# Layer 0 attention: row maxima carried by VectorE's 32x32 transpose and four small DMAs, in place of a TensorE transpose and a subtraction

## The chip, the cores and the metric

The kernel runs on one core of one Trainium2 chip. The metric is the device time of one execution in microseconds. Before the change it is 1144.48 us, the median of three runs (1144.44 to 1144.59).

The engines are named as in the profile: PE is TensorE's matrix multiplication and PEld its load of weights, DVE is VectorE, ACT is ScalarE, POOL is GpSimd, and SP is the engine whose queue issues most DMAs. A name such as L702 is line 702 of the kernel.

## What is computed

A transformer of two layers over x of 4 sequences x 512 tokens x 256 features, in float32. Layer 0 is causal attention with 16 heads of size 16, and then a feed-forward part that weighs the two best of eight experts for each output feature. Layer 1 is attention over the batch axis and a gated feed-forward part with 4-bit weights. The change touches layer 0's attention alone:

```python
qkv = einsum('bsd,od->bso', layernorm(x), w_project)      # 16 heads of 16, 512 keys
att = einsum('bhqd,bhkd->bhqk', q, k) / sqrt(16)
att = where(causal, -1e9, att)                            # a query sees keys up to its own
att = softmax(att, axis=-1)                               # needs the greatest score of each row
out = einsum('bhqk,bhkd->bhqd', att, v)
x = x + einsum('bsd,od->bso', out, w_out)
```

## The kernel before

The 512 tokens of a sequence are cut into 4 blocks j of 128. Queries and keys lie feature-major in one tile `qk[partition, g, block, s, token]`. The 16 heads are 4 groups g of 4 heads h, head h of a group lies in the band of partitions 32h to 32h+31, and s is the sequence. Places 0 to 3 of the block axis hold the keys of the four blocks; places 4 and 5 hold the queries of block j at place 4 + j % 2. In a band the 16 features lie at rows 4 to 19. Row i (0 to 3) of the keys of group i is 1 and the other rows outside the features are 0; the rows of the queries outside the features start at 0. These rows are set by GpSimd: once for block 0 (L496, a copy of a 0/1 mask spread over 4x512 columns), for later blocks by `blank` (L491), and for the queries by two fills with 0 (L500, and L521 in `blanks`).

The attention is worked through in 44 batches (j, s, groups): 4 batches of four groups for j = 0, 8 of two groups for j = 1, 16 of one group for j = 2, and 16 of one group for j = 3. Each batch has these steps:

- `greatest(n)`, L683: the scores with queries along partitions, into four PSUM tiles (one for each head h), by matmuls over the 32 rows of a band, four bands at a time.
- `mask(n)`, L696 and L702: a bf16 product adds -1e30 at later keys, and four VectorE reductions take each row's maximum into `maxes` (128 queries x head x group).
- `shift(n)`, L712 and L715: TensorE transposes `maxes` into a PSUM tile, so that row 32h + g holds the maxima of head h of group g along the columns. VectorE then subtracts this whole tile from the queries of the batch's groups. Row g of the queries now holds minus the maximum, and since the keys of group g have 1 in that row, the next product gives score minus maximum.
- `powers(n)`, L731, L740 and L750: the scores again, now with keys along partitions, over the same 32 rows, so that the maximum is already taken off. ScalarE takes the exponential, and GpSimd clears later keys in the last block.
- `mixed(n)`, L767: the product with the values, into a PSUM tile of the pool `ps_mm` (one buffer, which the transposed maxima use too), copied out by ScalarE.
- `divided`: the division by the sum, the projection and the addition to x.

The scores of both kinds take their four tiles from `ps_sc`, a pool of five buffers. So `powers(n)` can write its second tile only when the reductions of batch n+1 have freed theirs.

The main loop emits for batch n: `greatest(n+1)`, `shift(n)`, `mask(n+1)`, other work, `mixed(n-1)`, `powers(n)`, other work. "Other work" is taken by `fill` from streams of pieces: projections of later blocks, and the whole feed-forward part of layer 0 (L249 router and expert products on TensorE; L386 to L441 the choice of the two best, L365 to L367 additions, all on VectorE). How much is taken is fixed while the program is written out, from a cost that each piece states, and not from real times. TensorE, VectorE, ScalarE and GpSimd then keep that order. SP keeps it only up to batch 3; after that its order is set by the scheduler's priorities, and the four steps of a batch have a raised one.

SP issues, in the early batches, the DMAs that move projected queries and keys from `stage` to `qk` (L564, eight for each half block, 64 KB each) and the loads of the weights `rw` and `ew` of the experts (256 KB each). A DMA waits for an earlier DMA of the same of eight semaphores, eight DMAs back.

At the start, TensorE runs ten matmuls on an identity (L831) while x arrives. GpSimd sets the rows of `qk`, builds two small constants, and takes the inverse roots for the first layer norm (L649).

Of the kernel before, what the change touches and what calls it, by code (L numbers as in the profile page):

```python
# [8 lines left out]
F32 = mybir.dt.float32  # L9
# [3 lines left out]
ALU = mybir.AluOpType  # L13
# [3 lines left out]
P = 128  # L17
# [4 lines left out]
NBLK = 4  # L22
# [10 lines left out]
def tile_transformer(  # L33
# [18 lines left out]
    nc = tc.nc  # L52
# [23 lines left out]
    ident = const.tile([P, P], F32, name="ident")  # L76
# [9 lines left out]
    mask32 = const.tile([P, 32], F32, name="mask32")  # L86
# [16 lines left out]
    b2 = w_ffn0.enter_context(tc.tile_pool(name="f0_2", bufs=2, side="right"))  # L103
# [360 lines left out]
    with ExitStack() as l0:  # L464
        w0 = l0.enter_context(tc.tile_pool(name="w_l0", bufs=1))
        a1 = l0.enter_context(tc.tile_pool(name="l0_1", bufs=1))
# [3 lines left out]
        ps_mm = l0.enter_context(tc.tile_pool(name="l0_mm", bufs=1, space=PSUM))  # L470
# [5 lines left out]


        qk = w0.tile([P, 4, NBLK + 2, NS, P], F32, name="qk")
        maxes = [w0.tile([P, 4, 32], F32, name=f"mx{i}") for i in range(2)]

        va = w0.tile([P, NBLK * NS * NH0 * 17 + 15], F32, name="va")
        per_block = NS * NH0 * 17
# [2 lines left out]
        def blank(j, i):  # L485

            if i == 4:
                to = va.shape[1] if j == NBLK - 1 else (j + 1) * per_block
                nc.gpsimd.memset(va[:, j * per_block : to], 1.0)
            else:  # L490
                nc.gpsimd.tensor_copy(  # L491
                    qk[:, i, j].rearrange("p s q -> p (s q)"),
                    mask32[:, i : i + 1].to_broadcast([P, 512]),
                )

        nc.gpsimd.tensor_copy(  # L496
            qk[:, :, 0].rearrange("p g s q -> p g (s q)"),
            mask32[:, :4].unsqueeze(2).to_broadcast([P, 4, 512]),
        )
        nc.gpsimd.memset(qk[:, :, NBLK].rearrange("p g s q -> p g (s q)"), 0.0)  # L500

        ident_h = w0.tile([P, P], BF16, name="ident_h")
        nc.gpsimd.tensor_copy(ident_h, ident)
# [3 lines left out]
            out=later, in_=later, compare_op=ALU.is_ge, fill=NEG,  # L507
# [3 lines left out]
        rows = b1.tile([P, 12, P], BF16, tag="part", name="rows")  # L511
        sel = rows[:, :8]
        bp = rows[:, 8:].rearrange("p i q -> p (i q)")

        def blanks(xn):

            after = b2.tile([P, 1], F32, tag="rs_v", name="after")
            nc.gpsimd.tensor_copy(after, xn[:, 3, 0:1])
            for i in range(2):
                nc.gpsimd.memset(maxes[i], 0.0)  # L520
            nc.gpsimd.memset(qk[:, :, NBLK + 1].rearrange("p g s q -> p g (s q)"), 0.0)  # L521

        def split_biases():

# [24 lines left out]
        def project(j, xT, half, stage, i):  # L549

            at = 256 * (1 - i) + 128 * half
            ps = ps_dn.tile([P, 512], F32, tag="dn", name=f"qk_ps{j}_{half}_{i}")
            for hc in range(2):
                nc.tensor.matmul(  # L554
                    ps, lhsT=wp[:, hc, at : at + P],
                    rhs=xT[:, hc].rearrange("p s q -> p (s q)"), start=hc == 0, stop=hc == 1,
                )
            (nc.scalar.copy if j or not half else nc.vector.tensor_copy)(stage[:, i], ps)
            if i:
                to = 4 + j % 2  # L560
                for r in range(8):
                    h = 32 * (r % 4)
                    eng = nc.scalar if j == 0 and r % 2 else nc.sync
                    eng.dma_start(  # L564
                        out=qk[h + 4 : h + 20, 2 * half + r // 4, j : to + 1 : to - j].rearrange(
                            "p i s q -> p i (s q)"
                        ),
                        in_=stage[16 * r : 16 * r + 16],
                    )
# [95 lines left out]
        for j in range(NBLK):  # L665
            n = (4, 2, 1, 1)[j]
# [5 lines left out]
        def queries(j, g):  # L672
            return qk[:, g, 4 + j % 2]

        def greatest(n):

            j, s, gs = batches[n]
            nk = (j + 1) * P
            tiles = [ps_sc.tile([P, 512], F32, tag="sc", name=f"s1_{n}_{h}") for h in range(4)]
            for b, g in enumerate(gs):  # L680
                for h in range(4):
                    r = slice(32 * h, 32 * h + 32)
                    nc.tensor.matmul(  # L683
                        tiles[h][:, b * nk : (b + 1) * nk].rearrange("p (c k) -> p c k", k=P),
                        lhsT=queries(j, g)[r, s], rhs=qk[r, g, : j + 1, s, :],
                        start=b == 0, stop=False,
                    )
            open_scores[n] = tiles

        def mask(n):  # L690

            j, s, gs = batches[n]
            nk, nb = (j + 1) * P, len(gs)
            tiles = open_scores.pop(n)
            for ps in tiles:
                nc.tensor.matmul(  # L696
                    ps[:, : nb * nk].rearrange("p (b k) -> p b k", b=nb)[:, :, j * P :],
                    lhsT=ident_h, rhs=later.unsqueeze(1).to_broadcast([P, nb, P]),
                    start=False, stop=True,
                )  # L700
            for h, ps in enumerate(tiles):
                nc.vector.tensor_reduce(  # L702
                    maxes[n % 2][:, h, gs[0] : gs[0] + nb],
                    ps[:, : nb * nk].rearrange("p (b k) -> p b k", b=nb), AX.X, ALU.max,
                )

        def shift(n):


            j, s, gs = batches[n]  # L710
            ps = ps_mm.tile([P, P], F32, tag="mm", name=f"mxT_{n}")
            nc.tensor.transpose(ps, maxes[n % 2].rearrange("p h g -> p (h g)"), ident)  # L712
            g, nb = gs[0], len(gs)
            q = qk[:, g : g + nb, 4 + j % 2, s, :]
            nc.vector.tensor_tensor(  # L715
                q, q, ps.unsqueeze(1).to_broadcast([P, nb, P]), ALU.subtract
            )

        powers_of = {}

        def powers(n):

            j, s, gs = batches[n]
            nk, nb = (j + 1) * P, len(gs)
            tiles = [ps_sc.tile([P, 512], F32, tag="sc", name=f"s2_{n}_{h}") for h in range(4)]
            for b, g in enumerate(gs):
                for c in range(j + 1):
                    at = b * nk + c * P
                    for h in range(4):
                        r = slice(32 * h, 32 * h + 32)  # L730
                        nc.tensor.matmul(  # L731
                            tiles[h][:, at : at + P],
                            lhsT=qk[r, g, c, s, :], rhs=queries(j, g)[r, s],
                            start=True, stop=True,
                        )
            powers_of[n] = []
            for pair in range(2):
                pt = a3.tile([P, 2, 512], F32, tag="pt", name=f"pt_{n}_{pair}")
                for i in range(2):
                    nc.scalar.activation(  # L740
                        pt[:, i, : nb * nk], tiles[2 * pair + i][:, : nb * nk], AF.Exp, scale=0.25
                    )

                last = pt[:, :, : nb * nk].rearrange("p h (b k) -> p h b k", b=nb)[
                    :, :, :, j * P :
                ]
                pattern = [[0, 2], [0, nb], [1, P]]
                if nb == 1:
                    last, pattern = last[:, :, 0], [[0, 2], [1, P]]
                nc.gpsimd.affine_select(  # L750
                    out=last, in_=last, compare_op=ALU.is_ge, fill=0.0,
                    base=0, pattern=pattern, channel_multiplier=-1,
                )
                powers_of[n].append(pt)
# [74 lines left out]
        ps = ps_mm.tile([P, 4, P], F32, tag="mm", name="idle")  # L829
        for i in range(5):  # L830
            nc.tensor.matmul(  # L831
                ps, lhsT=ident, rhs=ident.unsqueeze(1).to_broadcast([P, 4, P]),
# [2 lines left out]
        load_x(1)  # L835
        nc.sync.dma_start(out=wo, in_=w_out.rearrange("(k p) o -> p k o", p=P))
        xn = normed_by_twos()
        blanks(xn)
        xT = a1.tile([P, 2, NS, P], F32, tag="xT0", name="xT0_0")
        for piece in inputs_T(0, xn, xT):  # L840
            pass
# [25 lines left out]
        for piece in inputs_T(1, second[0], xT):  # L867
            pass
        greatest(0)
        mask(0)  # L870
        inputs = {1: Stream(projections(1, xT))}
        done = blanked = 0
        fold = Stream(fold_pieces())
# [4 lines left out]
        for n in range(NBT):  # L878
            j, s, gs = batches[n]
            if n in (1, 7):  # L880
                to = 2 if n == 1 else 3
# [5 lines left out]
            with tc.high_priority(offset=AHEAD):  # L887
                if n + 1 < NBT:
                    greatest(n + 1)
                shift(n)  # L890
                if n + 1 < NBT:
                    mask(n + 1)

            fill(PE=(2.0, 2.0, 1.8, 1.6)[j], DVE=2.6)
            with tc.high_priority(offset=AHEAD):
# [73 lines left out]
    with ExitStack() as l1:  # L969
# [3 lines left out]
        for kv, i in [(slice(None), slice(HPK + 1, HPK + 2))] + [  # L973
            (slice(kv, kv + 1), slice(0, HPK + 1)) for kv in range(NKV)
        ]:
            for hc in range(2):
                tc.keep_in_program_order(
                    nc.sync.dma_start(
                        out=wqkv[:, hc, kv, i], in_=w_qkv[hc * P : (hc + 1) * P, kv, i]
# [239 lines left out]
        for p in range(-1, NP):  # L1219
            j, kv = divmod(p, NKV)  # L1220
# [59 lines left out]
    with ExitStack() as f1:  # L1280
# [186 lines left out]
        f, k = firsts  # L1467
# [3 lines left out]
        for i in range(NBLK * NJ):  # L1471
            j, jj = divmod(i, NJ)
# [12 lines left out]
            e, g = eg[:, 0], eg[:, 1]  # L1485
# [147 lines left out]
```

## Time and profile before

The profiled execution took 1144.61 us. Its span, from the first to the last instruction, is 1142.9 us.

| stretch (us) | what runs there | PE busy | DVE busy | POOL busy |
|---|---|---|---|---|
| 20 to 120 | blocks 0 and 1, projections, loads of expert weights | 97.88 of 100 | 68.13 | 34.12 |
| 120 to 160 | block 2 begins, experts fill in | 40.00 of 40 | 34.96 | 8.81 |
| 160 to 360 | blocks 2 and 3 with experts | 197.06 of 200 | 185.20 | 36.04 |
| 360 to 1143 | rest of the experts, layer 1 | 760.33 of 783 | 543.27 | 152.69 |

A busy PE in these rows is one on which some matmul is in flight; it includes time in which the next matmul waits behind the last, so 100% doesn't say that TensorE alone sets the time. The granted clock is 1.00 in every stretch. The steps of the change run from 22 us (first L683) to 366 us (last L731).

| step | instruction | count | mean or median ns |
|---|---|---|---|
| L683 | matmul over 32 rows, 128 to 512 columns | 512 | 287 to 639 |
| L696 | mask product, bf16, 128 columns a group | 176 | 219 at one group |
| L702 | reduction of 384 or 512 columns | 176 | 548, 681 |
| L712 | transpose of the maxima | 44 | 327 |
| L715 | subtraction | 44 | 281, 418 or 690 for one, two, four groups |
| L731 | matmul over 32 rows, 128 columns | 1280 | 287 |
| L767 | product with the values | 1280 | 276 |

### The profile page before, as it was taken

The page shows a single profiled execution, that of the slowest core. Times are in us where ns is not written, and L with a number is a line of the kernel's source. Part 1 is how long each engine was busy: PE and PEld are TensorE (multiplying, and loading weights), DVE is VectorE, ACT ScalarE, POOL GpSimd, SP SyncE. Part 2 cuts the span into 40 slices and gives each one's busy share as a digit, 9 for nine tenths or more (in the row PEclk, how much of TensorE's full clock was granted, in tenths as well). Part 3 has the DMA queues.
Part 4 walks back from the last instruction along what each step waited for, and adds up shares of the span by engine and source line. Part 5 has one row for each costly group of instructions (what it writes and reads, how often), then busy time and mean ns, then how long its engine had stood idle before and what let it go on. Part 6 is the DMA issues. An engine that isn't in the chain of part 4 may idle for free.

```text
span 1142.9 us, 19523 instructions
## 1 busy us (share of the span) xinstructions
PE 1113.0 (97%) x7474; PEld 716.1 (63%) x7474; DVE 844.6 (74%) x1856; ACT 509.8 (45%) x1190; POOL 247.1 (22%) x319
## 2 busy tenths in 40 slices
PE   9999999999999999999999999999999999999998
PEld 5666555555555445555555556656787788888885
DVE  6676989999988962867772695577479877778665
ACT  1445545565555543444444353344324444444442
POOL 8322221211112000000000000000064544353433
PEclk9999999999999999999999999999999999999999
DMA  4450110000000400000000001242001002002000
GB/s 133 113 130 2 21 20 1 2 1 2 1 2 1 156 29 1 1 1 1 1 1 0 1 1 38 65 111 65 20 1 45 30 19 74 1 19 74 18 3 19
DMA packets 30510, 34.92 MB, mean 31 GB/s; under 512 B 4280, under 2 KB 21432, under 8 KB 30416
## 3 DMA queue, kind: packets, MB, share of 16 engines
q1 hardware_dynamic: 29600, 32.49, 10.4%
q10 hardware_dynamic: 816, 1.18, 0.4%
q8 instruction: 59, 0.97, 0.3%
q14 instruction: 35, 0.29, 0.1%
HBM read 23.17 MB, written 6.29 MB: 26 GB/s over the span
## 4 chain that ended last, share of the span: by engine, by line
PE 69%; DVE 22%; ACT 3%; issue 2%; POOL 1%; SPq 1%; DMA 1%; DVEq 0%; POOLq 0%; ACTq 0%
PE qk_ps L1029 10%; PE lg_ps L249 9%; PE o L1120 8%; PE eo L249 7%; PE eg L955 7%; PE gu_first L955 5%; PE s L731 3%; PE yx L1336 3%; DVE mx L702 3%; PE s L683 3%; PE av L767 2%; PE yy L1336 2%; DVE it L1412 2%; DVE th L1411 2%; PE qk_ps L554 2%
## 5 line engine op out<-in xcount | busy, mean ns | idle before, releaser
L1029 PE MATMUL qk_ps<-xT,wqkv 128*128 128x512 f32 x320 | 148.7, 599 | 3.5 <-ACT v L1015 1.7
L249 PE MATMUL lg_ps<-rw,xT 128*128 128x512 f32 x256 | 122.5, 601 | 1.4 <-ACT xT L996 0.3
L249 PE MATMUL eo<-ew,xT 128*128 128x512 f32 x256 | 121.5, 600 | 0.8 <-ACT lg L312 0.5
L1120 PE MATMUL o<-wpj,oT 128*128 128x256 f32 x512 | 119.1, 382 | 0.0
L750 POOL TENSOR_SCALAR_AFFINE_SELECT pt<-pt 128x256 f32<-128x256 f32 (+2 forms) x88 | 62.4, 716 | 246.6 <-ACT pt L740 246.5
L1120 PEld LDWEIGHTS o<-wpj,oT 128*128 128x128 f32 x512 | 96.0, 190 | 27.0 <-issue 13.5
L1029 PEld LDWEIGHTS qk_ps<-xT,wqkv 128*128 128x128 f32 x320 | 59.1, 190 | 73.2 <-issue 58.4
L702 DVE TENSOR_REDUCE mx<-s 128x1 f32<-128x384 f32 (+3 forms) x176 | 100.4, 632 | 0.0
L740 ACT ACTIVATE pt<-s 128x512 f32<-128x512 f32 (+1 forms) x176 | 84.1, 564 | 35.8 <-PE s L731 35.8
L182 POOL TENSOR_TENSOR ln_rs<-rs_v,minus_half 128x4 f32<-128x4 f32 x12 | 13.6, 1131 | 366.2 <-DVE rs_v L181 366.2
L338 ACT ACTIVATE part<-eo,c 128x256 f32<-128x256 f32 x128 | 53.6, 472 | 84.6 <-PE eo L249 74.7
L1523 ACT COPY gu_first<-eg 128x512 f32<-128x512 f32 x28 | 16.0, 570 | 134.2 <-PE eg L955 129.9
L249 PEld LDWEIGHTS lg_ps<-rw,xT 128*128 128x128 f32 x256 | 46.1, 190 | 46.1 <-issue 37.3
L249 PEld LDWEIGHTS eo<-ew,xT 128*128 128x128 f32 x256 | 46.1, 190 | 45.7 <-issue 38.3
L312 ACT COPY lg<-lg_ps 128x512 f32<-128x512 f32 x64 | 37.7, 588 | 73.5 <-PE lg_ps L249 73.5
L1314 POOL TENSOR_TENSOR it<-it 128x512 f32<-128x512 f32 x30 | 38.2, 1273 | 146.6 <-PE gu_first L955 66.9
L1033 ACT COPY qT<-qk_ps 128x512 f32<-128x512 f32 x64 | 37.5, 586 | 64.7 <-PE qk_ps L1029 64.7
L1336 PE MATMUL yx<-it,wd 128*128 128x256 f32 x240 | 66.2, 379 | 0.0
L683 PE MATMUL s<-qk 32*128 32x128 f32 (+3 forms) x512 | 56.8, 465 | 0.2
L438 DVE SCALAR_TENSOR_TENSOR junk<-lg,w 128x256 bf16<-128x256 f32 x128 | 55.1, 430 | 0.0
L365 DVE TENSOR_TENSOR part<-part 128x512 f32<-128x512 f32 x32 | 22.5, 704 | 43.9 <-ACT part L338 43.9
L731 PE MATMUL s<-qk 32*128 32x128 f32 x1280 | 54.4, 287 | 0.5
(306 smaller groups left out, 2231.9 us busy)
## 6 DMA issues: line engine op xcount, KB each, us to landing
qk<-stage SPq DMA_DIRECT2D x56, 64.0 KB, 2.4
wqkv<-in_w_qkv SPq DMA_DIRECT2D x8, 320.0 KB, 7.1
rw<-in_router_w SPq DMA_DIRECT2D x8, 256.0 KB, 4.7
ew<-in_expert_w SPq DMA_DIRECT2D x8, 256.0 KB, 5.3
wpj<-in_w_proj SPq DMA_DIRECT2D x1, 2048.0 KB, 11.0
dq_sgu<-in_gate_up_s SPq DMA_DIRECT2D x64, 32.0 KB, 2.1
xres<-in_x SPq DMA_DIRECT2D x3, 512.0 KB, 4.8
xT_rows<-xT SPq DMA_DIRECT2D x12, 128.0 KB, 2.4
```

What stands on the lines that cost most here:

```text
L249: nc.tensor.matmul(ps, lhsT=xT[:, hc, (g % 4) * P : (g % 4 + 1) * P], rhs=w[:, hc, 2 * pair : 2 * pair + 2, :].rearrange("p e o -> p (e o) ...
L338: nc.scalar.mul(part[:, e % 4], ps[:, i], c[:, e : e + 1])
L438: stt(junk, d[:, e], 0.0, w1, ALU.is_gt, ALU.mult, accum_out=c1[:, e : e + 1])
L683: nc.tensor.matmul(tiles[h][:, b * nk : (b + 1) * nk].rearrange("p (c k) -> p c k", k=P), lhsT=queries(j, g)[r, s], rhs=qk[r, g, : j + 1, ...
L702: nc.vector.tensor_reduce(maxes[n % 2][:, h, gs[0] : gs[0] + nb], ps[:, : nb * nk].rearrange("p (b k) -> p b k", b=nb), AX.X, ALU.max,)
L731: nc.tensor.matmul(tiles[h][:, at : at + P], lhsT=qk[r, g, c, s, :], rhs=queries(j, g)[r, s], start=True, stop=True,)
L740: nc.scalar.activation(pt[:, i, : nb * nk], tiles[2 * pair + i][:, : nb * nk], AF.Exp, scale=0.25)
L750: nc.gpsimd.affine_select(out=last, in_=last, compare_op=ALU.is_ge, fill=0.0, base=0, pattern=pattern, channel_multiplier=-1,)
L955: nc.tensor.matmul(ps[:, w], lhsT=lhs(w), rhs=rhs, start=start and not i and not w, stop=i == len(terms) - 1 and w == 1, skip_group_check= ...
L1029: nc.tensor.matmul(ps, lhsT=wqkv[:, hc, kv, h, :], rhs=xT[:, hc, :], start=hc == 0, stop=hc == 1,)
L1120: nc.tensor.matmul(ys[t // 2][:, t % 2], lhsT=state["o"][:, h, t * P : (t + 1) * P], rhs=wpj[:, HPK * kv + h, :], start=kv == 0 and h == 0 ...
L1336: nc.tensor.matmul(ps, lhsT=lhs(jj), rhs=its[8 * j + jj][:, plane], start=start and not n, stop=n == 1, skip_group_check=not start,)
```

## The change

The features now lie at rows 0 to 15 of a band, and row 16 carries the maximum. GpSimd sets whole blocks of the keys to -1 by fills, and the feature rows are then written over by the DMAs from `stage`. The queries' rows are no longer set beforehand: the first scores read rows 0 to 15 alone and the second read rows 0 to 16. `maxes` is one tile in place of two, laid out as group x 32, so that VectorE's transpose of 32x32 blocks puts the maxima of head h of a group at partition 32a + h for the queries 32a to 32a+31. Four DMAs on SP's queue, one for each a, take four partitions of the result to row 16 of the four bands of the queries. Each moves 4 rows of 32 floats a group, which is 2 KB at four groups and 512 bytes at one.

The transpose of the maxima on TensorE and the subtraction on VectorE are gone. `shift(n+1)` now comes right behind `mask(n+1)`, so it is emitted one batch before the `powers` that uses it, and `shift(0)` stands ahead of the loop. The mask product is unchanged.

```diff
-        maxes = [w0.tile([P, 4, 32], F32, name=f"mx{i}") for i in range(2)]
+        maxes = w0.tile([P, 4, 32], F32, name="mx")
+        nc.vector.memset(maxes, 0.0)
...
-                nc.gpsimd.tensor_copy(
-                    qk[:, i, j].rearrange("p s q -> p (s q)"),
-                    mask32[:, i : i + 1].to_broadcast([P, 512]),
-                )
-
-        nc.gpsimd.tensor_copy(
-            qk[:, :, 0].rearrange("p g s q -> p g (s q)"),
-            mask32[:, :4].unsqueeze(2).to_broadcast([P, 4, 512]),
-        )
-        nc.gpsimd.memset(qk[:, :, NBLK].rearrange("p g s q -> p g (s q)"), 0.0)
+                nc.gpsimd.memset(qk[:, i, j].rearrange("p s q -> p (s q)"), -1.0)
+
+        nc.gpsimd.memset(qk[:, :, 0].rearrange("p g s q -> p g (s q)"), -1.0)
...
-        def blanks(xn):
-
-            after = b2.tile([P, 1], F32, tag="rs_v", name="after")
-            nc.gpsimd.tensor_copy(after, xn[:, 3, 0:1])
-            for i in range(2):
-                nc.gpsimd.memset(maxes[i], 0.0)
-            nc.gpsimd.memset(qk[:, :, NBLK + 1].rearrange("p g s q -> p g (s q)"), 0.0)
...
-                        out=qk[h + 4 : h + 20, 2 * half + r // 4, j : to + 1 : to - j].rearrange(
+                        out=qk[h : h + 16, 2 * half + r // 4, j : to + 1 : to - j].rearrange(
...
-                    r = slice(32 * h, 32 * h + 32)
+                    r = slice(32 * h, 32 * h + 16)
...
-                    maxes[n % 2][:, h, gs[0] : gs[0] + nb],
+                    maxes[:, :nb, h],
...
-            ps = ps_mm.tile([P, P], F32, tag="mm", name=f"mxT_{n}")
-            nc.tensor.transpose(ps, maxes[n % 2].rearrange("p h g -> p (h g)"), ident)
             g, nb = gs[0], len(gs)
-            q = qk[:, g : g + nb, 4 + j % 2, s, :]
-            nc.vector.tensor_tensor(
-                q, q, ps.unsqueeze(1).to_broadcast([P, nb, P]), ALU.subtract
+            mT = a1.tile([P, 4, 32], F32, tag="mT", name=f"mT_{n}")
+            nc.vector.transpose(
+                mT[:, :nb].rearrange("p b q -> p (b q)"),
+                maxes[:, :nb].rearrange("p b h -> p (b h)"),
             )
+            for a in range(4):
+                nc.sync.dma_start(
+                    out=qk[16:P:32, g : g + nb, 4 + j % 2, s, 32 * a : 32 * a + 32],
+                    in_=mT[32 * a : 32 * a + 4, :nb],
+                )
...
-                        r = slice(32 * h, 32 * h + 32)
+                        r = slice(32 * h, 32 * h + 17)
...
-        blanks(xn)
...
         mask(0)
+        shift(0)
...
                 if n + 1 < NBT:
                     greatest(n + 1)
-                shift(n)
                 if n + 1 < NBT:
                     mask(n + 1)
+                    shift(n + 1)
```

The tile `mT` has one buffer. In the built program the transpose of batch n+1 waits for the four DMAs of batch n, each of the four waits for a DMA eight back, and the first matmul of `powers(n)` waits for the four DMAs of its batch. The order of all other instructions on TensorE, VectorE, ScalarE and GpSimd is the same. On SP the DMAs of the maxima stand between those of `stage` and the loads of `rw` and `ew`.

## The prediction

> **What bounds the kernel now.** I read the page first: busy shares and the chain that ended last.
>
> ```profile
> PE 1113.0 (97%) x7474; PEld 716.1 (63%) x7474; DVE 844.6 (74%) x1856; ACT 509.8 (45%) x1190; POOL 247.1 (22%) x319
> PE 69%; DVE 22%; ACT 3%; issue 2%; POOL 1%; SPq 1%; DMA 1%; DVEq 0%; POOLq 0%; ACTq 0%
> ```
>
> TensorE carries most of the chain, VectorE a fifth, and DMA next to nothing. Then the chain in order of time, in two stretches, because the batches differ. Columns are start, length, piece.
>
> ```profile
> 63.27 1.07 PE s L683 x16
> 64.34 0.26 PE mxT L712
> 64.60 0.44 PE s L696 x4
> 65.04 0.22 PE oq_T L802 x2
> ...
> 241.60 0.27 PE mxT L712
> 241.88 0.02 issue
> 241.90 0.29 DVE qk L715
> 242.19 2.39 DVE mx L702 x4
> ...
> 249.36 0.20 DVE qk L715
> 249.55 2.40 DVE mx L702 x4
> ```
>
> At 64 us the transpose is a link of an unbroken TensorE chain: its 0.26 us is paid. At 241 us the chain leaves TensorE through transpose and subtraction into VectorE, and at 249 us it stays on VectorE, which pays 0.20 for the subtraction. I summed the chain's pieces from 20 to 400 us: L712 is on it 33 times with 7.9 us (10 times before 130 us, 23 after), L715 14 times with 3.4 us: six entries of 0.29 and eight of 0.20.
>
> **The change, part by part.**
>
> *A. GpSimd at the start.* The chain there goes through the copy L496 and the fill L500:
>
> ```profile
> 1.92 1.88 POOL qk L496
> 3.80 1.74 POOL qk L500
> ...
> 6.28 1.51 POOL ln_rs L649 x2
> ```
>
> One fill of the same size (1.80 busy) remains, so GpSimd is ready for the roots about 2 us sooner. They then wait for VectorE, whose L648 took 0.79 us beside the fill and 0.17 after it, and L644 0.71 against 0.39: it wins 0.9 back. L521 (1.80) goes too. VectorE's new fill of `maxes` lies in its 1.73 us wait for x and costs nothing there; without that wait it costs about 0.1 (1024 columns took 0.91). TensorE's ten idle matmuls end at 8.45 whatever GpSimd does, so the gain may be 0; at best it is 1.3 (0.9 and less contention in L191, 2.52 us for four). I take -0.8, since the chain from 14 to 25 us is mostly VectorE.
>
> *B. The TensorE transpose.* 0.26 each. Early: 10 on the chain, -2.3. Late: 23, of which 6 enter VectorE (under C); the other 17 carry 4.0 us. VectorE is 185.2 of 200 us busy from 160 to 360, so a faster TensorE soon meets it: I keep half, -2.0 (ends: 0 and -4.0). A further 11 transposes off the chain count 0, at best -2.9. Fewer rows (32 to 16 or 17) I cost at 0: weight loads over 32 rows take 186 ns and over 128 rows 190, so rows hardly matter.
>
> *C. Six entries.* From the transpose to the reductions is 0.59 us (241.60 to 242.19). Afterwards the reductions wait for the first mask product instead, 0.22 long and some 0.04 later: 0.33 saved each, -2.0 (ends: 0 if VectorE is late anyway, and -2.4).
>
> *D. VectorE's transpose for the subtraction.* Its price isn't shown at 32 columns. The nearest rows:
>
> ```profile
> L1051 DVE STREAM_TRANSPOSE sm<-s 128x512 f32<-128x512 f32 x16 | 11.4, 715 | 24.1 <-PE s L1042 24.1
> L209 DVE STREAM_TRANSPOSE xT<-xn 128x1024 f32<-128x1024 f32 x3 | 3.7, 1238 | 0.0
> L715 DVE TENSOR_TENSOR qk<-qk,mxT 128x128 f32<-128x128 f32 x32 | 9.0, 281 | 15.0 <-PE mxT L712 14.9
> ```
>
> With 713 and 1220 ns (means over both kinds of transposes) a line gives 0.99 ns a column and 0.24 us at 32. It must follow the last reduction (0.03, as between L177 and L178), where the subtraction took 0.20 from its start to the next: +0.07. Five waits need two extra queue entries (the subtractions with five and nine waits left six of 50 ns): +0.07 of their 0.10. So +0.14 a batch, on the eight batches that stay on VectorE: +1.1. Ends: 0.06, the shortest VectorE instruction here, makes it -0.11 a batch; 0.33, the line at 128 columns, and full entries +0.26.
>
> [...]
>
> *E. Waits on TensorE.* `powers(n)` waits for four DMAs: two entries of 51 ns before its first weight load. Four such entries in L683 at 122.8 us left it at 0.86 us, the same as at 160 us without: end 0. The other end is 0.15. I take 0.05 on the 27 batches under B: +1.3. Behind this wait stand all later matmuls; `mixed` stands ahead of it and no longer waits for the subtraction.
>
> *F. The DMAs.* 176 more, each past SP's queue. The window, and the nearest DMAs:
>
> ```profile
> 176.85 1.94 DVE L702 TENSOR_REDUCE mx<-s 128x1 f32<-128x384 f32 x4
> ...
> 184.48 1.42 PE L731 MATMUL s<-qk 32*128 32x128 f32 x23
> ```
>
> ```profile
> 67.67 14.91 SPq L564 DMA_DIRECT2D qk<-stage  x16
> ...
> 781.24 3.58 SPq L929 DMA_DIRECT2D dq_sd<-in_down_s  x8
> ```
>
> ```profile
> ew<-in_expert_w SPq DMA_DIRECT2D x8, 256.0 KB, 5.3
> dq_sd<-in_down_s SPq DMA_DIRECT2D x32, 32.0 KB, 1.8
> ```
>
> From the last reduction of a batch (178.79) to its `powers` (184.48) are 5.7 us; this and 5.6 (344.59 to 350.22) are the shortest of the steady batches, most have 6 to 9, and batch 0 has 5.1. Needed: transpose 0.24, SP 0.07 (a stage copy ended at 67.60, its DMA issued at 67.67), three issues of 0.45 (3.58 for eight), landing 1.8 to 2.4 (64 KB): 3.5 to 4.1. I cost F at 0; what hides it is a whole batch of other products. The upper end, 0.93 an issue (14.91 for 16) and 5.3 to land, is 8.4, or 2.7 us late a batch.
>
> The loads are worst at batch 4: its DMAs stand behind 1 MB of `ew` and 0.5 MB of x. Issued from 59.5, they land by 66.2 even at 5.3; `powers(4)` is at 68.13. Stage DMAs behind the maxima go 1.8 later: block 1's second half by about 60, first used at 63.2. The single `mT` makes a transpose wait for DMAs a batch old, which VectorE would feel, and behind it all fill work, only if they took over 5 us.
>
> [...]
>
> **Sum.** -0.8 - 2.3 - 2.0 - 2.0 + 1.1 + 1.3 = -4.7. From the profiled 1144.6 (span 1142.9 and 1.7 around it) that is 1139.9; the median is 0.1 lower: 1139.8.
>
> **Rivals.** What the measurement can tell from no change is 0.2%, 2.3 us.
>
> *VectorE takes the gain.* It is 93% busy from 160 to 360, and 27 batches there add 3.8 us. Against: it still waits for L712 there (10.5 us). Late B and C fall to 0, D counts on 19 batches (+2.7): -0.8 - 2.3 + 2.7 + 1.3 = +0.9, 1145.4.
>
> *TensorE gains everywhere.* The value products' weight loads waited 27.2 us on VectorE (L702 18.9, L715 8.3), through the PSUM buffer shared with the transposed maxima; that wait goes. All 44 transposes then count, -11.4, A -1.3, C -0.4 for what it saves beyond its transposes, D and E 0: -13.1, 1131.4. Against: `powers` still needs the same reductions for its buffers.
>
> *The maxima land late (slower).* Place: first matmul of `powers`, with all of TensorE behind it. It decides once a transfer's whole path passes about 5.6 us, and mostly above 6.5. At 7.0, about 20 late batches wait 0.7 on average: +14 - 4.7, 1154. For it: eight-back waits and 0.93 issues. Against: from 90 to 360 SP and the rings have little else, and 32 KB landed in 1.8.
>
> **How the numbers follow.** Forecast 0.53 (own range 1136 to 1142.2), everywhere 0.15, VectorE 0.17, late 0.15. So faster 0.68, same 0.17, slower 0.15. The range goes from the everywhere case, 1131, to the VectorE case with E at its upper end (27 times 0.10 more), 1148; outside lies most of the late case.
>
> **What would show it.** No L712; in TensorE-bound batches L696 follows L683 directly and the batch is 0.26 shorter. VectorE's transpose near 0.24. First matmul of `powers` waits on no DMA; if the view of waits names the maxima's DMA ahead of L720, F was wrong. VectorE's share from 160 to 360 rises to about 96%. Roots at the start about 1 us sooner.

## The result and the profile after

The changed kernel takes 1148.3 us, the median of 13 runs (1143.8 to 1152.28); the kernel before, run on the same chip, takes 1144.48 (1144.42 to 1144.75, 13 runs). The ratio is 1.0034, with a 95% interval of 1.002 to 1.0048. So the change makes the kernel slower by 3.8 us, where the forecast was 4.7 us faster; 1148.3 lies 0.3 above the range. The spread has grown as well, from 0.3 us to 8.5.

The page of the profiled execution, the slowest of the 13 at 1152.28 us, has its first surprise in a row that the prediction had taken as constant: the granted clock of TensorE, in 40 slices of the span.

```profile
span 1150.6 us, 19771 instructions
PE 1120.2 (97%) x7430; PEld 716.1 (62%) x7430; DVE 843.1 (73%) x1857; ACT 509.2 (44%) x1190; POOL 240.2 (21%) x314
PEclk8999997999999999999999999999999999999999
PE 69%; DVE 22%; ACT 4%; issue 2%; DMA 1%; POOL 1%; SPq 1%; DVEq 0%; ACTq 0%; POOLq 0%
```

TensorE has 44 matmuls less (the transposes) and is busy 7.2 us longer. The clock row has an 8 and a 7, where the row of before had nines throughout. VectorE and DMA have their old shares of the chain, so the maxima's way is not what has become slow. The stretches of the table of before, with the clock in the eighth column (window, its length, busy PE, PEld, DVE, ACT, POOL, clock):

```profile
20.00:120.00 100.00, 98.46 (x1100) 65.27 (x1102) 62.02 (x130) 40.17 (x79) 32.04 (x47) 0.94 0.33 81
120.00:160.00 40.00, 40.00 (x432) 22.16 (x432) 34.09 (x78) 20.99 (x56) 8.92 (x11) 1.00 0.17 28
160.00:360.00 200.00, 197.88 (x2049) 105.01 (x2048) 181.49 (x437) 114.47 (x313) 34.27 (x54) 0.94 0.01 2
360.00:1150.00 790.00, 768.74 (x3824) 516.84 (x3824) 550.83 (x1179) 330.08 (x741) 153.26 (x181) 1.00 0.10 29
```

All the missing clock lies in the first 357 us, at the start and where layer 0's attention runs. The clock events of the trace show it as stretches at half clock: 6.8 us at 18.5, then 3.4 at 32.2, 3.4 at 93.6, 10.2 at 172.1, 3.4 at 196.0, 226.7 and 257.4, and 3.4 at 353.0. Each is a multiple of 3.413 us; together they are 37.5 us. What precedes one of them is seen in the timeline of PE (start, length, group; x counts two records for each float32 product: the 640 products of L720 are 1280 in the trace):

```profile
188.49 1.98 PE L249 MATMUL lg_ps<-rw,xT 128*128 128x512 f32 x4
190.40 0.93 PE L669 MATMUL s<-qk 16*128 16x384 f32 x8
191.26 0.40 PE L682 MATMUL s<-later,ident_h 128*128 128x128 bf16 x4
191.59 0.86 PE L756 MATMUL av<-pt,va 128*32 128x128 f32 x24
192.38 1.51 PE L720 MATMUL s<-qk 17*128 17x128 f32 x23
...
193.96 2.15 PE L669 MATMUL s<-qk 16*128 16x384 f32 x7
196.04 0.61 PE L682 MATMUL s<-later,ident_h 128*128 128x128 bf16 x4
196.44 3.42 PE L249 MATMUL lg_ps<-rw,xT 128*128 128x512 f32 x4
```

TensorE is never idle here: a matmul is in flight all the time. But from 190.4 to 196.0 there is no float32 product over 128 rows and 128 columns; the work is attention's, over 16 or 17 rows, or into 32 columns. At 196.0 the clock is halved, and the same four products of L249 that took 1.98 us take 3.42.

The second surprise is at the start. The timeline after, GpSimd, VectorE and TensorE together:

```profile
13.69 1.92 POOL L492 MEMSET qk<- 128x512 f32 x4
13.78 5.02 DVE L191 TENSOR_SCALAR xn<-xres,ln_mv,ln_rs 128x256 f32<-128x256 f32 x4 [1.19 <-POOL ln_rs L182]
15.55 1.00 POOL L490 MEMSET va<- 128x1088 f32 x1
16.50 0.52 POOL L515 MEMSET rows<- 128x512 bf16 x1
...
19.44 0.79 PE L562 MATMUL v_ps<-wp,xT 128*128 128x256 f32 x1 [3.16 <-DVE stage L544]
```

And the same place before:

```profile
14.10 2.46 POOL L491 COPY qk<-mask 128x512 f32<-128x512 f32 x4
14.18 2.52 DVE L191 TENSOR_SCALAR xn<-xres,ln_mv,ln_rs 128x256 f32<-128x256 f32 x4 [1.12 <-POOL ln_rs L182]
```

Beside copies of GpSimd the four L191 take 2.52 us. Beside fills they take 5.02: the first alone lasts 3.39 us, to 17.2, just behind the end of the last fill at 17.0. TensorE then waits 3.16 us for VectorE (the bracket is idle time and its releaser), and its next products run at half clock. The first scores begin at 27.43 in place of 22.44, 5.0 us late. The fills alone don't make 5.0: in the profile of experiment 2 below, with the same fills and the same 3.39 us but no halved stretch, the first scores begin at 24.17. Over the batches the 5.0 grows to 9.1 at batch 43. Between two halved stretches most batches gain 0.15 or 0.16; a batch with a halved stretch of 3.4 us loses 0.2 to 1.7, and the one with the stretch of 10.2 loses 4.2.

### The profile page after: what moved, and what is told of

Read it like the earlier page. It is cut to its first block, busy times and chain, and to the rows that moved or that the text cites. A ratio compares the mean times of both kernels' runs of the same rounds, so it can differ in the third digit from the quotient of the medians.

```text
span 1150.6 us, 19771 instructions
## 1 busy us (share of the span) xinstructions
PE 1120.2 (97%) x7430; PEld 716.1 (62%) x7430; DVE 843.1 (73%) x1857; ACT 509.2 (44%) x1190; POOL 240.2 (21%) x314
## 4 chain that ended last, share of the span: by engine, by line
PE 69%; DVE 22%; ACT 4%; issue 2%; DMA 1%; POOL 1%; SPq 1%; DVEq 0%; ACTq 0%; POOLq 0%
PE qk_ps L1018 10%; PE lg_ps L249 9%; PE o L1109 8%; PE eo L249 7%; PE eg L944 7%; PE gu_first L944 5%; PE yx L1325 3%; PE s L720 3%; PE s L669 3%; DVE mx L688 3%; PE av L756 2%; PE yy L1325 2%; DVE it L1401 2%; DVE th L1400 2%; PE qk_ps L540 2%
## 5 line engine op out<-in xcount | busy, mean ns | idle before, releaser
L249 PE MATMUL lg_ps<-rw,xT 128*128 128x512 f32 x256 | 127.0, 620 | 1.4 <-ACT aT L794 0.4
L249 PE MATMUL eo<-ew,xT 128*128 128x512 f32 x256 | 124.7, 613 | 1.1 <-ACT lg L312 0.5
L249 PEld LDWEIGHTS lg_ps<-rw,xT 128*128 128x128 f32 x256 | 47.4, 195 | 48.2 <-issue 39.3
L249 PEld LDWEIGHTS eo<-ew,xT 128*128 128x128 f32 x256 | 47.2, 194 | 47.6 <-issue 39.8
L1022 ACT COPY qT<-qk_ps 128x512 f32<-128x512 f32 x64 | 37.5, 585 | 64.7 <-PE qk_ps L1018 64.7
L669 PE MATMUL s<-qk 16*128 16x128 f32 (+3 forms) x512 | 55.9, 464 | 0.2
L720 PE MATMUL s<-qk 17*128 17x128 f32 x1280 | 54.2, 289 | 0.5
```

Of the source, the lines that this page charges most:

```text
L249: nc.tensor.matmul(ps, lhsT=xT[:, hc, (g % 4) * P : (g % 4 + 1) * P], rhs=w[:, hc, 2 * pair : 2 * pair + 2, :].rearrange("p e o -> p (e o) ...
L669: nc.tensor.matmul(tiles[h][:, b * nk : (b + 1) * nk].rearrange("p (c k) -> p c k", k=P), lhsT=queries(j, g)[r, s], rhs=qk[r, g, : j + 1, ...
L720: nc.tensor.matmul(tiles[h][:, at : at + P], lhsT=qk[r, g, c, s, :], rhs=queries(j, g)[r, s], start=True, stop=True,)
```

## The experiments

The theory (R) was that the number of rows a product contracts over counts for whether TensorE's clock is halved behind it, although it hardly changes how long a matmul takes: 289 ns over 17 rows after the change, 287 over 32 before. The rivals were that the missing transposes thin TensorE's work out (T), and that the late start by GpSimd's fills (S) does the harm. In the diffs "before" and "after" name the kernel that is edited.

**1. The rows alone, in the kernel before.** Features lie at rows 4 to 19 there, so 20 rows hold everything that isn't zero in the queries.

```diff
 (before, both products)
-                    r = slice(32 * h, 32 * h + 32)
+                    r = slice(32 * h, 32 * h + 20)
```

> The kernel before with one edit: both score products contract over 20 rows of a band in place of 32 (rows 20 to 31 are zero on both sides, so nothing is left out). Theory R (active rows count towards the clock: with fewer rows a stretch of 3.41 us in which TensorE also waits falls under the threshold, and the clock is halved): four to eight such stretches between 80 and 345 us, granted clock about 0.985 to 0.993, 1148 to 1155 us. Theory I (only TensorE's idle time counts, rows don't): the same as before, 1144.5 us, clock 1.00.

Measured: 1149.01 (1147.44 to 1150.05, 5 runs), ratio 1.0037, interval 1.0024 to 1.005. Nothing else was touched: transposes, subtraction and start are those of before. In its windows the clock falls where after's falls:

```profile
160.00:200.00 40.00, 39.55 (x377) 21.75 (x373) 36.24 (x94) 21.86 (x61) 9.80 (x13) 0.91 0.01 1
200.00:240.00 40.00, 40.00 (x370) 19.77 (x364) 36.52 (x87) 22.80 (x64) 6.78 (x10) 0.96 0.01 2
240.00:280.00 40.00, 40.00 (x416) 21.85 (x419) 36.65 (x88) 23.23 (x66) 5.26 (x10) 0.96 0.01 2
```

Halved stretches stand at 24.7 (6.83 us), 171.4, 191.9, 222.6 and 253.4 (3.41 each). The stretch at 222.6 can be laid beside the kernel before. Here is the same batch, first before and then with 20 rows, each with the window that follows:

```profile
214.47 0.86 PE L767 MATMUL av<-pt,va 128*32 128x128 f32 x24
215.27 0.95 PE L731 MATMUL s<-qk 32*128 32x128 f32 x24
216.04 2.47 PE L683 MATMUL s<-qk 32*128 32x384 f32 x8
218.00:221.40 3.40, 3.40 (x36) 1.60 (x33) 3.40 (x7) 0.91 (x3) 2.02 (x2) 1.00 0.00 0
```

```profile
218.17 0.86 PE L767 MATMUL av<-pt,va 128*32 128x128 f32 x24
218.96 0.95 PE L731 MATMUL s<-qk 20*128 20x128 f32 x24
219.74 2.47 PE L683 MATMUL s<-qk 20*128 20x384 f32 x8
222.60:226.00 3.40, 3.40 (x6) 0.93 (x4) 3.37 (x9) 0.00 (x0) 1.11 (x1) 0.51 0.00 0
```

The pieces are equally long and TensorE is in flight throughout; only the rows differ, and the rows left out hold zeros. Behind 32 rows the clock stays at 1.00, behind 20 it is halved. So R is shown with one factor: fewer rows alone cost 4.5 us. By what rule rows count is not shown.

**2. The rows given back, in the kernel after.** All 32 rows are read again. For that the queries must be zero outside the features, which takes two GpSimd fills behind the first layer norm.

```diff
 (after)
-                    r = slice(32 * h, 32 * h + 16)
+                    r = slice(32 * h, 32 * h + 32)
...
-                        r = slice(32 * h, 32 * h + 17)
+                        r = slice(32 * h, 32 * h + 32)
...
+        def blanks(xn):
+
+            after = b2.tile([P, 1], F32, tag="rs_v", name="after")
+            nc.gpsimd.tensor_copy(after, xn[:, 3, 0:1])
+            for to in (NBLK, NBLK + 1):
+                nc.gpsimd.memset(qk[:, :, to].rearrange("p g s q -> p g (s q)"), 0.0)
...
+        blanks(xn)
```

> The changed kernel with both score products over 32 rows again, and the queries' rows set to 0 by two GpSimd fills at the start, behind the first layer norm; the maxima in row 16 stay in the first scores of blocks 2 and 3, which moves all of a row's scores by one number that the softmax takes out. Theory R: the halved stretches from 80 us on are gone, those at the start stay; clock 0.995 or more, 1148.3 less some 7 is about 1141. Theory I: the stretches stay, about 1148 us.

Measured: 1142.29 (1139.83 to 1145.38, 10 runs), ratio 0.9983, interval 0.9971 to 0.9995. The profiled execution has no halved stretch (span 1139.6), although the first L191 takes 3.39 us again. So 6.0 us of the result came back with the rows, and with them the sign of the change.

**3. The start given back.** GpSimd writes -1 by copies from a column, as it wrote the mask before; the rows stay at 16 and 17.

```diff
 (after)
         nc.vector.memset(maxes, 0.0)
+        minus_one = w0.tile([P, 1], F32, name="minus_one")
+        nc.vector.memset(minus_one, -1.0)
...
-                nc.gpsimd.memset(qk[:, i, j].rearrange("p s q -> p (s q)"), -1.0)
+                nc.gpsimd.tensor_copy(
+                    qk[:, i, j].rearrange("p s q -> p (s q)"),
+                    minus_one.to_broadcast([P, 512]),
+                )
```

> The changed kernel with the later key blocks set to -1 by GpSimd copies of one column, as before, in place of fills. Theory S (GpSimd's fills keep VectorE's second layer norm waiting, so TensorE idles 3.2 us at 16 us and its clock is halved): the four L191 instructions take 2.5 us in place of 5.0, the first scores start near 22 us in place of 27.4, 1148.3 - 5 is about 1143 us; the halved stretches from 80 us on stay. If the start's loss has another cause: 1148 us.

Measured: 1147.22 (1146.03 to 1149.64, 8 runs), ratio 1.0023, interval 1.0012 to 1.0034. The cause at the start is right: each L191 takes 676 to 695 ns and the first scores begin at 22.02, 5.4 us earlier than after the change. But by the medians the end comes only 1.1 us earlier, not the 5 that were expected: clock 0.987 to 0.989, with six halved stretches of 27.3 us in all. Part of this is which execution was profiled: the one after the change is the slowest of its 13, and against it the profiled one here (1147.32) ends 5.0 earlier. How the start goes in the faster executions after the change no profile shows, so the price of the fills at the end stays open.

**4. Both given back:** the edits of experiments 2 and 3 together.

> Both edits together. Theories R and S: no halved stretch after the first 6 us, clock 1.00, and what is left is the change's own gain, some 5 to 8 us: 1136 to 1140 us. If rows don't count, 1143 us; if the transposes that were taken out are what kept the clock up, stretches remain and 1140 to 1144 us.

Measured: 1142.67 (1139.6 to 1144.16, 10 runs), ratio 0.9978, interval 0.9968 to 0.9988. Against experiment 3, the rows are worth 4.6 us here. 1136 to 1140 and a clock of 1.00 were expected, and only the best execution is there; most of the others lie in the 1140 to 1144 that was expected under T, which experiment 6 tests. Two halved stretches are left in the profile, at 24.3 and 171.1. Windows at the second:

```profile
164.30:167.70 3.40, 3.40 (x52) 2.27 (x40) 3.00 (x8) 2.11 (x6) 1.82 (x3) 1.00 0.01 3
167.70:171.10 3.40, 2.33 (x15) 1.37 (x14) 3.37 (x9) 0.58 (x2) 1.12 (x1) 1.00 0.00 0
171.10:174.50 3.40, 3.40 (x51) 2.52 (x50) 3.33 (x9) 1.28 (x4) 0.00 (x0) 0.50 0.02 5
```

In the middle one TensorE is busy for 2.33 of 3.40 us: it waits 1.06 us for VectorE's `oq`. The window after it runs at 0.50. The kernel before is busy for 3.70 of the 4 us from 166 to 170.

**5. More work at the start.** To experiment 4 come one unused matmul on the identity (512 columns) ahead of `greatest(0)` and four behind `mask(0)`.

```diff
+        idle = ps_mm.tile([P, 4, P], F32, tag="mm", name="idle_zero")
+        for i in range(1):
+            nc.tensor.matmul(
+                idle, lhsT=ident, rhs=ident.unsqueeze(1).to_broadcast([P, 4, P]),
+                start=not i, stop=i == 0,
+            )
         greatest(0)
         mask(0)
         shift(0)
+        idle = ps_mm.tile([P, 4, P], F32, tag="mm", name="idle_first")
+        for i in range(4):
+            nc.tensor.matmul(
+                idle, lhsT=ident, rhs=ident.unsqueeze(1).to_broadcast([P, 4, P]),
+                start=not i, stop=i == 3,
+            )
```

> The kernel of the run with 32 rows and copies, with five more matmuls on the identity (0.43 us each, result unused) in the first batches: one before greatest(0), four behind mask(0), where TensorE waits 0.7 us for a DMA and some 1.7 us for the first reductions. Theory R says that the halving at 24 us comes from these waits: it goes, clock 0.998 or more, some 2 to 3 us less than without them, 1139 to 1141 us. If the loss of the start doesn't come from the clock: 1143 us or more.

Measured: 1143.66 (1142.64 to 1144.9, 11 runs), ratio 0.9988, interval 0.9979 to 0.9997: a miss. The halved stretch at 24 is gone, but others stand at 93.1 and 171.6, and five matmuls of 0.9 to 1.0 us, where 0.43 was expected of each, lie on TensorE's path.

**6. The transposes put back, unused** (theory T). To experiment 4 comes an unused transpose in every batch where L712 stood.

```diff
+                spare = ps_mm.tile([P, P], F32, tag="mm", name=f"spare_{n}")
+                nc.tensor.transpose(spare, ident, ident)
```

> The same 32 rows and copies, with a TensorE transpose of the identity into the unused buffer wherever the transpose of the maxima stood; nothing waits for it. It prices the removed transposes: by the prediction's B and C 27 to 33 of the 44 lie on the path at 0.26 us, so 4 to 8 us more than without them if the clock is the same. Theory T (the missing transposes lower the clock too): the last halved stretches go, clock 1.00 in every run and a spread below 1 us; the two effects then nearly cancel, 1142 to 1145 us. Theory R alone: the stretches stay as without them, 1146 to 1149 us.

Measured: 1144.39 (1143.44 to 1146.17, 10 runs), ratio 0.9998, interval 0.9989 to 1.0007, clock 0.997 to 1.000. The time lies within the 1142 to 1145 that was expected under T, but T's signs, a clock of 1.00 in every run and a spread below 1 us, are missing. The halved stretch at 171 is absent from its profile, and the lowest clock is 0.997 where experiment 4 has 0.995, so some effect of the transposes on the clock isn't excluded. But the median is 1.7 above experiment 4's: as a means to keep the clock up the transposes cost more than they keep. And their absence isn't what slowed the kernel after, since experiment 4 lacks them too and is faster than the kernel before. Executions at clock 1.000 took 1143.4 and 1143.7, and experiment 4's only one took 1139.6: by these three, 44 transposes are worth about 3.9 us at full clock.

**7 and 8. Which product's rows.** Experiment 4 with 17 rows in `powers` alone, and with 16 rows in `greatest` alone.

```diff
 (experiment 7, in powers)
-                        r = slice(32 * h, 32 * h + 32)
+                        r = slice(32 * h, 32 * h + 17)
 (experiment 8, in greatest)
-                    r = slice(32 * h, 32 * h + 32)
+                    r = slice(32 * h, 32 * h + 16)
```

> 32 rows in the first scores, 17 in the second, copies as before. Theory R: rows of either product count by their TensorE time. The second scores have 54 us of matmul time against 57 of the first (the page's groups), so each should bring back about half of the halved stretches: clock 0.992 to 0.997, 1143 to 1146 us, and the same for the other half. If rows don't count: as with 32 rows in both, 1142.7 us.

> 16 rows in the first scores, 32 in the second, copies as before. Theory R: about half of the halved stretches, clock 0.992 to 0.997, 1143 to 1146 us. The first scores stand where TensorE waits for ScalarE's and VectorE's buffers, so if a waiting matmul counts, theirs should matter more than those of the second scores.

Measured: 1142.68 (1139.51 to 1146.9, 10 runs), ratio 0.9985, interval 0.9971 to 0.9998; and 1143.68 (1140.21 to 1148.51, 10 runs), ratio 0.9991, interval 0.9976 to 1.0005. Of both, 1143 to 1146 was expected. By the medians the first can't be told from experiment 4. The clock of the executions can: it goes down to 0.991 and 0.990, where experiment 4 never fell below 0.995. So each product alone brings executions with more halved time than with all rows. The split of the 4.6 us between the two stays open.

**9. One matmul, meant for the place where TensorE waited.** To experiment 2 comes one unused matmul on the identity, 512 columns, behind the mask product of batch 17.

```diff
                     shift(n + 1)
+                if n == 16:
+                    idle = ps_mm.tile([P, 4, P], F32, tag="mm", name="idle_16")
+                    nc.tensor.matmul(
+                        idle, lhsT=ident, rhs=ident.unsqueeze(1).to_broadcast([P, 4, P]),
+                        start=True, stop=True,
+                    )
```

> The kernel of 32 rows with fills, plus one unused identity matmul of 512 columns behind the mask product of batch 17, the place near 168 us where TensorE waits 0.5 to 1.1 us for VectorE. It leaves nothing out. If the halved stretch at 171 us that several variants show is set by too little work in the window before it, that stretch goes in all executions; executions at 1145 become rare, and the median falls from 1142.3 to about 1141.5 (the matmul itself costs up to 0.4). If the halved stretch has nothing to do with this place, the clock stays spread from 0.996 to 1.000 and the median goes up by 0.4, to 1142.7.

Measured: 1141.4 (1139.68 to 1142.6, 5 runs), ratio 0.9963, interval 0.9951 to 0.9976. No execution is above 1142.6, where four of ten stood at 1144.1 to 1145.4 in experiment 2; the profiled one has only a stretch at 19.2, beside the fills of the start. Five executions are few, though: at four in ten, five without one have a chance of 8%. And the matmul isn't where it was meant to be. It runs from 162.45 to 163.53, but the wait stands behind the mask product of batch 18, 0.63 us from 167.47 in the profile of experiment 2. Here that wait is gone: TensorE comes later to the place, and VectorE's `oq` is ready.

**10. The cover of the four DMAs taken away.** Experiment 2 with `shift(n)` back where it stood before the change, ahead of the reductions of batch n+1.

```diff
-        shift(0)
...
                     greatest(n + 1)
+                shift(n)
                 if n + 1 < NBT:
                     mask(n + 1)
-                    shift(n + 1)
```

> The kernel of 32 rows with fills, with the transpose and the four DMAs of batch n back at the place of the old subtraction: ahead of the reductions of batch n+1, not behind those of batch n. It leaves nothing out. In the trace of the 32-row kernel the first reduction of batch n+1 starts 0.2 to 4.3 us ahead of the powers of batch n, 2.1 in the median. If the maxima need 3.1 to 3.4 us from the transpose (three issues of 0.50 and 1.6 to 1.9 to land), the powers wait 42 to 52 us in sum over the batches; 25 if they need only 2.5. So 1167 to 1195, with a wait for the maxima's DMA ahead of the powers. If the DMAs are nearly free wherever they stand, the time stays within 1140 to 1147.

Measured: 1178.3 (1174.17 to 1179.94, 4 runs), ratio 1.0281, interval 1.0259 to 1.0303. What ended the idle time ahead of the powers (L727 here; us, times), and who waited for the DMAs (L710):

```profile
  DMA qk<-mT: 43.9, 25
...
L710 SPq DMA_DIRECT2D qk<-mT x176: 497/497/684, 27.8 to 397.5; - x176
  PE s L727: 38.0, 22
  PEld s L727: 11.4, 6
```

The waits named are 44 to 49 us, where 42 to 52 were expected from the windows; the time rises by 36. The clock falls as well, to 0.985 to 0.993, with six halved stretches of 30.7 us in the profile, each behind a window in which TensorE waited; what the waits alone would cost isn't parted from this. The first line of the second group gives the shortest, median and longest issue on SP. So the transfers are not cheap. They are hidden, and the place of `shift` is what hides them.

**11. Two matmuls against the two stretches.** To experiment 4 come the matmul of experiment 9 and the one ahead of `greatest(0)` of experiment 5; both diffs are above.

> The kernel of 32 rows with copies, plus the same unused matmul behind the mask product of batch 17, and one ahead of the first scores, where TensorE waited 0.69 us for a stage DMA. It leaves nothing out. If the remaining halved stretches (24.3 us, 6.83 long, and 171.1 us, 3.41 long) come from too little work in the windows at 20.9 and 167.7, both go: profile clock 1.00 and 1139.5 to 1141.5. If only the place at 168 is decided by it, the clock is 0.997 and the time 1141 to 1143. If neither, 1143 to 1145.

Measured: 1139.8 (1139.51 to 1140.22, 5 runs), ratio 0.9953, interval 0.994 to 0.9965: faster than both kernels, and with a spread of 0.7 us. The windows shown for experiment 4 are now

```profile
164.30:167.70 3.40, 3.28 (x20) 1.91 (x19) 3.33 (x8) 1.90 (x5) 1.64 (x3) 1.00 0.01 3
167.70:171.10 3.40, 3.40 (x56) 2.36 (x57) 3.37 (x8) 1.88 (x5) 0.00 (x0) 1.00 0.02 5
171.10:174.50 3.40, 3.40 (x12) 1.39 (x14) 3.37 (x13) 2.29 (x7) 0.98 (x2) 1.00 0.01 1
```

Two useless matmuls of about 1 us bring 2.9 us, and the profile has no halved stretch. The first, at 21.92, does fill the window before the old stretch at 24.3. The second runs from 159.75 to 160.83, seven microseconds ahead of the window that was to be filled; what changed there is that the wait for `oq` is 0.1 us long, not 1.06, and that other work falls into the window. What each of the two brings alone was not run on this kernel.

## Why the prediction was wrong, by its steps

**The step that failed** is in part B: "Fewer rows (32 to 16 or 17) I cost at 0: weight loads over 32 rows take 186 ns and over 128 rows 190, so rows hardly matter." The reading of the duration was right, as the groups after the change show (busy, mean ns):

```profile
L720 PE MATMUL s<-qk 17*128 17x128 f32 x1280 | 54.2, 289 | 0.5
L698 DVE STREAM_TRANSPOSE mT<-mx 128x32 f32<-128x32 f32 x32 | 6.8, 212 | 1.1
```

289 ns over 17 rows, against 287 over 32. What the step left out is that the clock itself answers to the rows. It cost 4.5 us in experiment 1, 6.0 in experiment 2, and 4.6 between experiments 3 and 4. The whole sum stood on a clock of 1.00 that the page of before showed, and the prediction didn't ask what kept it there. Of the 8.5 us between forecast and result, 6.0 came back with the rows. The other 2.5 are not parted as cleanly: with all rows some executions still have halved stretches, behind windows in which TensorE waits, and experiment 2 still has the fills at the start. Experiment 11, without the fills and with no halved stretch in its profile, is at 1139.8.

**A, GpSimd at the start (-0.8): right for the roots, wrong beyond them.** The roots run at 5.25 and 6.52, the first a microsecond sooner. But the part looked at the first fills alone; the copies of L491 become fills too, and they lie beside L191, where I had counted on less contention. With copies in their place (experiment 4) the first scores begin at 21.96, 0.5 before the old 22.44. At the end the fills cost only 1.1 us by the medians (after against experiment 3), and in the 32-row kernels nothing that can be told (experiment 2 against 4). At a clock of 1.000 experiment 2 took 1141.3 to 1141.5 in three executions and experiment 4 1139.6 in its one, but experiment 9, with the fills too, took 1139.8 and 1141.5: what the fills cost at the end stays open.

**B, the transpose (early -2.3, late -2.0): the mechanism right, the price too high.** Timeline of PE before, and then in experiment 11, in the batch that the prediction showed:

```profile
63.20 1.15 PE L683 MATMUL s<-qk 32*128 32x256 f32 x16
64.27 0.33 PE L712 MATMUL mxT<-ident,mx 128*128 128x128 f32 x1
64.44 0.60 PE L696 MATMUL s<-later,ident_h 128*128 128x256 bf16 x4
```

```profile
62.91 1.15 PE L681 MATMUL s<-qk 32*128 32x256 f32 x16
63.99 0.61 PE L694 MATMUL s<-later,ident_h 128*128 128x256 bf16 x4
```

The mask product starts 1.24 us after the first scores before, and 1.08 after: 0.16 saved, not the 0.26 that the chain of waits put down for the transpose. The chain counts a link to its end; the next product had started 0.17 after the transpose did. In every batch but the first, the gap from the last scores to the mask product shrinks by 0.16 or 0.17. Experiment 11 starts its first scores 0.4 us late, is 1.1 ahead at batch 12 and 3.0 at batch 43: 1.5 us early, for a term of 2.3, and 1.9 from batch 12 on, all late terms together.

**C (-2.0): right in kind.** VectorE's wait for L712, 29.0 us in 14 waits, became 25.8 us in 14 waits for the mask product: 0.23 less each, where 0.33 was priced.

**D (+1.1): right.** The transpose takes 212 ns, where 240 was worked out, and 86 queue entries of 50 ns stand ahead of it, two a batch.

**E (+1.3): too high where it can be seen.** The 88 entries of 51 ns are there, but in the batch shown the powers start 1.01 us after the product with the values, before and in experiment 11 alike.

**F (0): right, and for the reason given.** The view of waits names the maxima's DMAs once after the change:

```profile
DVE mT L698 <- DMA qk<-mT: 0.4, 1, 0.4
```

No row of powers waits for them, not even in the batches behind the loads of the weights. Experiment 10 shows that the price of losing the cover is 36 us, the clock that the waits cost included, with the windows in the trace of experiment 2 giving the waits to within their range.

**The rivals.** "VectorE takes the gain": its share from 160 to 360 us is 186.68 of 200 in experiment 11, so neither full nor near the 96% that I named. "TensorE gains everywhere": the weight loads of the value products are still idle 27.9 us ahead of them, now put down to issue; that wait was not worth what I gave it. "The maxima land late" is experiment 10, and didn't happen in the kernel as changed.

The sum, 1139.8, is what experiment 11 measures. That is agreement of the whole, at a clock of 1.00, with terms that were off by 0.3 to 1.3 us, most of them too high on both sides of the sum, and with two added matmuls; that part is luck, and it doesn't make the terms right.

## What to carry to other kernels

Before a product is cut down in rows, or work on TensorE is taken away, look at the windows of 3.4 us, the length of the shortest halved stretch here, that hold only thin products, and at those in which TensorE waits. Full of products over 32 rows such a window kept the clock here (1.00 from 218.0 to 221.4 us in the kernel before); with 16 to 20 rows it often didn't (0.51 from 222.6 to 226.0 in experiment 1, behind the same products over 20 rows), and the full products behind it then ran at half clock, although each thin matmul took the same time as before (289 ns against 287). After adding work for the clock's sake, look in the timeline at where it went. Price a transfer by the cover of its place, and keep the two apart: the same four DMAs had one wait of 0.4 us to show in one place and, with the clock that waiting for them lost, cost 36 us in another. A link in the chain of pipelined matmuls was worth the distance to the next start, not its length: 0.17 us, not 0.26, for the transpose here.

## What the runs showed of the hardware

- **Rows count for the clock.** With 32 rows in a band the kernel before kept 1.00 in every stretch of its profile; with 20 it fell to 0.91 from 160 to 200 us with a matmul in flight for 39.55 of 40 us. TensorE needn't be idle for it: in the kernel after, the stretches at 93.6, 196.0, 226.7 and 257.4 us each follow 3.41 us in which a matmul was in flight throughout. The halved stretches of that trace, at a clock of 0.50, last 3.413, 6.827 and 10.240 us, and those at full clock between them 6.827 to 92.160, multiples of 3.413 too.
- **Two kinds of window go before a halved stretch.** With 32 rows in both products (experiments 2, 4, 5, 6, 9, 10 and 11, and before) every halved stretch up to 400 us follows a window of 3.41 us in which TensorE was busy for 2.55 us or less. With fewer rows in one product or both (after and experiments 1, 3, 7 and 8) 23 of 27 follow a window in which it was busy for 2.94 us or more. A threshold was not found: before has a window with 1.67 us, from 375.05 to 378.46, that the full clock survived.
- **The kernel with halved stretches spreads.** In the kernel after, the 13 executions go from 1143.8 us at a mean clock of 0.993 to 1152.3 at 0.984. The kernel before isn't free of it: of its 66 executions beside the experiments five had a clock of 0.997 or 0.998 and took 1146.1 to 1147.7.
- **A row of GpSimd's fills held VectorE's layer norm back at the start.** One L191 took 3.39 us there beside a row of fills, while before the change each took 0.68 to 0.70 beside copies of the same size and 0.40 to 0.42 with GpSimd idle. It isn't so beside every fill: after the change the L191 at 51.1 and 51.8 us, beside fills of L492, took 0.69 each.
